# Rounding the inner values of the feed-forward blocks to e5m2 on ScalarE in place of VectorE

## The chip, the cores and the metric

The kernel runs on one core of one Trainium2 chip. The core has five engines that work side by side and wait for each other through semaphores: TensorE (PE in the profile, PEld for its weight loads), VectorE (DVE), ScalarE (ACT), GpSimd (POOL) and SyncE (SP), which issues most DMAs. Each engine takes its instructions in the order in which they were written. The metric is the device time of one execution in microseconds; lower is better.

## The reference, cut to what matters

The model has two layers over 16 images of 48 x 48 pixels and 96 channels (2304 tokens an image). Each layer is a selective scan over the pixels in four directions, followed by a feed-forward block whose operands are rounded to an 8-bit float of 5 exponent and 2 mantissa bits (e5m2):

```python
EXP_MUL, MAN_MUL = (5, 2)
EXP_ACC, MAN_ACC = (5, 10)
q_mul = lambda x: _float_quantize(x, EXP_MUL, MAN_MUL)
q_acc = lambda x: _float_quantize(x, EXP_ACC, MAN_ACC)

def _qlinear(x, W, b):
    y = q_acc(jnp.einsum('bsk,nk->bsn', q_mul(x), q_mul(W)))
    return q_acc(y + q_mul(b))
h = jax.nn.relu(_qlinear(x, W1, b1))
y = _qlinear(h, W2, b2)
```

The inner values `h` have 384 channels a token. They are rounded to 16 bits after the product and after the bias, pass the relu, and are rounded to e5m2 (`q_mul`) as operand of the second product. That last rounding is what the change touches.

## The kernel before

**The scan.** The scans of all images and both layers make one long row of 9216 steps, laid out by `scans`. A step works on a tile of 128 rows by 768 pixels. ScalarE makes the decay `a` by an exp into PSUM (L633, two buffers), GpSimd makes `b` (L639), VectorE runs the scan (L696), the result is multiplied into `hc` (L700), and TensorE folds four `hc` tiles into the output (L663). `hc` has eight buffers. Where the scan's chunk is not the last of its direction, ScalarE copies the last column into `carry` (L706). In the order of the code, step n issues: pieces of other work, scan n (with its product), carry n, exp n+2, GpSimd's `b` of n+3, folds.

**Who multiplies.** The product at L700 goes to VectorE or to GpSimd. A ledger with one account an engine decides, step by step, before anything runs:

```python
here = load["gp"] + 2 * 1.82 > load["ve"] + 1.81 + SPARE
load["gp"] += 1.82 if here else 2 * 1.82
load["ve"] += 2.76 if here else 1.81
```

If `here`, VectorE scans in place and multiplies; otherwise it scans into another tile and GpSimd multiplies. Other work on the two engines enters its cost through `self.ve(us)` and `self.gp(us)`.

**The other work.** Everything besides the scan (norms, convolutions, projections, feed-forward) is written as generators that yield a weight after each piece. A phase is 288 steps; in it the generators of another image advance in proportion to the steps done. In half of the phases the other work is `middle` (the end of layer 0 and the start of layer 1 of an image); in the others it is `final` of one image (the end of layer 1) and `first` of another. After the last scan, the last image's `final` runs alone.

**The feed-forward block.** `feed_forward` (from L970) runs 18 items a block, three for each of six stretches of 384 tokens, as a pipe of three stages: `hidden` (L981, TensorE, into one of two PSUM buffers), `rounded` (L994 copies PSUM to 16 bits, L995 adds the bias and applies the relu in place, both on ScalarE) and `packed`, which after the third item of a stretch rounds the whole 128 x 3 x 384 tile `h1` into `hq` (L1000). `piped` calls the stages of one time in reverse, so that a stretch's `packed` is written ahead of the next stretch's first `rounded`. The second product (L1010) reads `hq`.

Of the kernel before, what the change touches and what calls it, by code (L numbers as in the profile page):

```python
# [16 lines left out]
AF = mybir.ActivationFunctionType  # L17
# [13 lines left out]
SUB = 384  # L31
# [106 lines left out]
class Net:  # L138
# [831 lines left out]
    def feed_forward(self, t, x):  # L970
        nc = self.nc
        w8, b1, b2 = self.ff[t]
        xn = yield from self.norm(x, 1e-5)
        xq = yield from self.channels_first(xn, F8, "xq")
        hq = self.bigt([128, 3, L], "hq", F8)
        h1 = {}

        def hidden(n, _):
            q, m = divmod(n, 3)
            o = self.pst()  # L980
            nc.tensor.matmul(  # L981
                o[:, :SUB],
                lhsT=w8[:DM, m * 128 : (m + 1) * 128],
                rhs=xq[:, q * SUB : (q + 1) * SUB],
                start=True,
                stop=True,
            )
            return o

        def rounded(n, o):  # L990
            q, m = divmod(n, 3)
            if m == 0:
                h1[q] = self.work.tile([128, 3, SUB], F16, name="h1", tag="w3")
            nc.scalar.copy(h1[q][:, m, :], o[:, :SUB])  # L994
            nc.scalar.activation(h1[q][:, m, :], h1[q][:, m, :], AF.Relu, bias=b1[:, m : m + 1])  # L995

        def packed(n, _):
            q, m = divmod(n, 3)
            if m == 2:
                nc.vector.tensor_copy(hq[:, :, q * SUB : (q + 1) * SUB], h1[q], saturate=False)  # L1000
                self.ve(1)

        yield from self.piped(3 * NQ, 0.8, hidden, rounded, packed, by=1)

        def product(q, _):
            o = self.pst()
            for i in range(TQ):
                at = (TQ * q + i) * 128
                for m in range(3):
                    nc.tensor.matmul(  # L1010
                        o[:, i * DM : (i + 1) * DM],
                        lhsT=hq[:, m, at : at + 128],
                        rhs=w8[:, HID + m * DM : HID + (m + 1) * DM],
                        start=(m == 0),
                        stop=(m == 2),
                    )
            return o

        y1 = self.bigt([128, NT, DM], "y1", F16)

        def half(q, o):
            nc.scalar.copy(self.rows(y1, q), o[:, : TQ * DM])

        yield from self.piped(NQ, 1, product, half)

        def biased(q, _):
            o = self.pst()
            nc.tensor.matmul(o[:, : TQ * DM], lhsT=self.ident16, rhs=self.rows(y1, q), start=True, stop=False)
            nc.tensor.matmul(o[:, : TQ * DM], lhsT=self.ones16, rhs=b2, start=False, stop=True)
            return o  # L1030

        yield from self.piped(NQ, 0.9, biased, half)

        def added(q, _):
            o = self.pst()
            nc.tensor.matmul(o[:, : TQ * DM], lhsT=self.ident, rhs=self.rows(x, q), start=True, stop=False)  # L1036
            nc.tensor.matmul(o[:, : TQ * DM], lhsT=self.ident16, rhs=self.rows(y1, q), start=False, stop=True)
            return o

        def put(q, o):  # L1040
            nc.scalar.copy(self.rows(x, q), o[:, : TQ * DM])

        yield from self.piped(NQ, 0.9, added, put)
# [171 lines left out]
```

## Time and profile before

| | |
|---|---|
| time, median of 3 runs | 26079.37 us (26070.98 to 26080.56) |
| the profiled execution's own time | 26086.89 us |
| its span, first to last instruction | 26085.1 us |
| mean granted TensorE clock | 0.754 |
| first scan starts at, last scan starts at | 221.8 us, 25878.7 us |
| L1000 on VectorE | 192 instructions, 259.0 us |
| idle time of VectorE just before L1000 | 138.9 us |
| L994 and L995 on ScalarE | 576 each, 269.8 and 354.0 us |
| ScalarE's table loads, each | 1.283 us |

The page gives the busy time of each engine and its share of the span. Such a share is a mean over stages with different limits. A group of instructions is told by its line, engine, operation and tiles; behind it stand its count, its busy time, the mean of one, and the idle time of the engine just before these instructions with what ended it. A window is a stretch of the span, in us from its start, with the busy time of each engine in it. A timeline lists instructions by their start, with the idle time before each and its releaser in square brackets.

### The profile page before, as it was taken

How to read it: one execution, taken by the hardware profiler on the slowest of the kernel's cores; microseconds unless marked ns; L12 is line 12 of the kernel's file. 1: busy time of each engine (PE TensorE's matmuls, PEld its weight loads, DVE VectorE, ACT ScalarE, POOL GpSimd, SP SyncE). 2: the span in 40 equal slices, each digit the busy share in tenths (PEclk: the TensorE clock that was granted, in tenths of full speed). 3: DMA queues.
4: the chain of work that ended last, by engine and by line, in shares of the span. 5: the costliest groups of instructions: out<-in, count | busy, mean ns of one | idle time of the engine just before them, and what ended most of it. 6: DMA issues, size and time to landing. Idle time of an engine off the chain costs nothing. (4 is left out here: it accounts for less than half of the span.)

```text
span 26085.1 us, 239798 instructions
## 1 busy us (share of the span) xinstructions
PE 18748.3 (72%) x70912; PEld 7359.5 (28%) x70912; DVE 22554.4 (86%) x16250; ACT 15281.8 (59%) x26690; POOL 22797.0 (87%) x13136
## 2 busy tenths in 40 slices
PE   6777667777677766777677866778766777667766
PEld 2223223222222222232222322223222332223222
DVE  6888888888888888888988889888888888988886
ACT  4566555666555565556655566655666555665554
POOL 6888889888888898888998889888899888988886
PEclk7777778777777777787777877778777877778776
DMA  5566566665566565665656656555665555665563
GB/s 194 217 220 224 200 220 227 222 221 209 213 221 222 218 216 209 217 224 219 227 205 218 220 218 231 206 211 219 222 228 216 206 215 221 231 220 204 211 228 140
DMA packets 1297666, 5614.99 MB, mean 215 GB/s; under 512 B 238176, under 2 KB 238176, under 8 KB 1277664
## 3 DMA queue, kind: packets, MB, share of 16 engines
q1 hardware_dynamic: 1219232, 5555.73, 58.4%
q10 hardware_dynamic: 77120, 43.93, 0.6%
q8 instruction: 558, 9.14, 0.1%
q14 instruction: 756, 6.19, 0.1%
HBM read 4707.93 MB, written 891.22 MB: 215 GB/s over the span
## 5 line engine op out<-in xcount | busy, mean ns | idle before, releaser
L639 POOL TENSOR_TENSOR b<-d,bc 128x768 f32<-128x768 f32 x9216 | 16488.9, 1813 | 733.4 <-DVE a L696 699.2
L633 ACT ACTIVATE a<-d,l_a 128x768 f32<-128x768 f32 x9216 | 8317.2, 904 | 3330.9 <-DVE hc L700 2437.2
L696 DVE TENSOR_TENSOR_SCAN a<-a,carry,b 128x768 f32<-128x768 f32 x4374 | 7924.9, 1812 | 887.4 <-ACT a L633 532.2
L663 PE MATMUL py<-hc,fold_sb 128*32 128x384 f32 x36864 | 6237.0, 644 | 2138.1 <-POOL hc L700 1457.3
L700 DVE TENSOR_TENSOR hc<-a,bc 128x768 f32<-128x768 f32 x6408 | 6138.7, 958 | 1254.7 <-PE py L663 637.2
L700 POOL TENSOR_TENSOR hc<-h,bc 128x768 f32<-128x768 f32 x2808 | 5089.8, 1813 | 1713.7 <-DVE h L696 1374.7
L696 DVE TENSOR_TENSOR_SCAN a<-a,b 128x768 f32<-128x768 f32 x2034 | 3557.8, 1749 | 484.6 <-ACT carry L706 244.9
L696 DVE TENSOR_TENSOR_SCAN h<-a,carry,b 128x768 f32<-128x768 f32 x1770 | 3192.2, 1807 | 161.2 <-ACT a L633 89.2
L706 ACT COPY carry<-a 128x1 f32<-128x1 f32 x4119 | 654.6, 159 | 4321.5 <-DVE hc L700 4309.9
L663 PEld LDWEIGHTS py<-hc,fold_sb 128*32 128x32 f32 x36864 | 1200.5, 125 | 6562.0 <-issue 2424.4
L329 PE MATMUL pst<-dts,wpack_sb 24*128 24x384 f32 x2304 | 1446.3, 772 | 1015.5 <-ACT dl L561 985.1
L696 DVE TENSOR_TENSOR_SCAN h<-a,b 128x768 f32<-128x768 f32 x1038 | 1809.6, 1746 | 72.1 <-ACT carry L706 69.8
L437 PE MATMUL pst<-e,dg 128*128 128x384 f32 x5184 | 1802.2, 497 | 0.0
L543 POOL TENSOR_TENSOR du<-dl,u 128x768 f32<-128x768 f32 x576 | 1043.6, 1812 | 598.5 <-DMA dd<-du 283.8
L437 PE MATMUL pst<-wxa,dg 128*128 128x384 f32 x3456 | 1219.2, 502 | 28.6 <-DMA dg<-taps_l1a 22.8
L437 PEld LDWEIGHTS pst<-e,dg 128*128 128x128 f32 x5184 | 952.2, 190 | 862.3 <-issue 267.3
L329 PE MATMUL pst<-xt,wpack_sb 96*128 96x384 f32 (+1 forms) x1536 | 805.7, 661 | 503.2 <-ACT wxb L472 273.2
L329 PEld LDWEIGHTS pst<-dts,wpack_sb 24*128 24x128 f32 x2304 | 587.0, 281 | 1890.2 <-ACT dl L561 1369.3
L651 PE MATMUL py<-first,l_skip 128*128 128x384 f32 x1152 | 689.9, 690 | 537.2 <-ACT yt L676 481.5
L651 PE MATMUL py<-first,ident 128*128 128x384 f32 x1152 | 711.3, 710 | 506.5 <-ACT yt L676 431.7
L329 PE MATMUL pst<-y,centre 128*128 128x384 f32 (+1 forms) x1536 | 853.7, 715 | 272.7 <-ACT y L937 223.8
L329 PE MATMUL pst<-u,wpack_sb 128*128 128x384 f32 (+1 forms) x2304 | 857.1, 518 | 188.7 <-ACT u L508 81.5
(167 smaller groups left out, 17714.6 us busy)
## 6 DMA issues: line engine op xcount, KB each, us to landing
bc<-bc SPq DMA_DIRECT2D x3072, 768.0 KB, 6.7
d<-dd SPq DMA_DIRECT2D x2304, 768.0 KB, 6.1
dd<-dl SPq DMA_DIRECT2D x192, 1152.0 KB, 8.0
dd<-du SPq DMA_DIRECT2D x576, 384.0 KB, 4.4
y<-yt SPq DMA_DIRECT2D x576, 384.0 KB, 2.4
u<-u SPq DMA_DIRECT2D x96, 1152.0 KB, 5.4
first<-u SPq DMA_DIRECT2D x288, 384.0 KB, 3.2
first<-y SPq DMA_DIRECT2D x288, 384.0 KB, 3.2
```

The source lines that it names most:

```text
L329: nc.tensor.matmul(img(o[: w.shape[1], :SUB]), lhsT=w, rhs=y, start=(k == 0), stop=(k == len(terms) - 1))
L437: nc.tensor.matmul(img(o[:, :SUB]), lhsT=dg[:n, k, :], rhs=img(p[:n], PW)[:, PQ * q + i : PQ * q + i + PQ, j : j + HW], start=(k == 0), st ...
L543: nc.gpsimd.tensor_tensor(du, dl[:, cs], u[j][:, cs], ALU.mult)
L633: nc.scalar.activation(a, of(n)[0][:, 0, :], AF.Exp, scale=rates[t][:, pair, j, i, g : g + 1])
L639: nc.gpsimd.tensor_tensor(b, d[:, 1, :], bc[:, 0, :], ALU.mult)
L651: nc.tensor.matmul(py[:, q, :SUB], lhsT=self.skip[t][:, j, :] if pair == 0 else self.ident, rhs=firsts[group][:, q * SUB : (q + 1) * SUB], ...
L663: nc.tensor.matmul(py[32 * k : 32 * k + 32, q, :SUB], lhsT=self.fold, rhs=(hcs[n + k] if q == 0 else hcs.pop(n + k))[:, q * SUB : (q + 1) ...
L696: nc.vector.tensor_tensor_scan(way(h), way(a), way(b), start, ALU.mult, ALU.add)
L700: (nc.vector if here else nc.gpsimd).tensor_tensor(hc, h, cc, ALU.mult)
L706: nc.scalar.copy(kept["carry"][:, at : at + 1], h[:, last : last + 1])
```

## The change

One instruction moves from VectorE to ScalarE. ScalarE's `activation` with `Identity` copies its input and rounds it to the type of the output, e5m2; it stands where VectorE's cast stood, and on ScalarE that is behind the relu that it reads and ahead of the next item's L994. The entry of 1 us in VectorE's account goes too, so that the ledger decides some later products otherwise.

```diff
         def packed(n, _):
             q, m = divmod(n, 3)
             if m == 2:
-                nc.vector.tensor_copy(hq[:, :, q * SUB : (q + 1) * SUB], h1[q], saturate=False)
-                self.ve(1)
+                nc.scalar.activation(hq[:, :, q * SUB : (q + 1) * SUB], h1[q], AF.Identity, saturate=False)
 
         yield from self.piped(3 * NQ, 0.8, hidden, rounded, packed, by=1)
```

## The prediction

> **What bounds the kernel now.** I read the page's busy shares first, then the groups by line and shape, then the windows of the stage that the diff touches, then the timeline inside one window. The chain of waits is not used: it accounts for 0% of the span on every engine.
>
> ```profile
> PE 18748.3 (72%) x70912; PEld 7359.5 (28%) x70912; DVE 22554.4 (86%) x16250; ACT 15281.8 (59%) x26690; POOL 22797.0 (87%) x13136
> ```
>
> VectorE (DVE) and GpSimd (POOL) share the load at 86% and 87%; ScalarE (ACT) looks free at 59%. But the change lives only where a feed-forward block makes its inner values, and there the shares differ. For each window below I took the stretch from an image's first L981 matmul to its last L995 relu: two from the first layer (the scan's middle phases), two from the second layer (with the next image's first part), then the two last images. Columns: length, then busy us (x instructions) of PE, PEld, DVE, ACT, POOL, clock, DMA share, GB/s.
>
> ```profile
> 7801.30:7845.60 44.30, 20.53 (x100) 5.08 (x97) 35.39 (x27) 32.62 (x64) 36.69 (x22) 0.62 0.37 135
> 8634.10:8676.00 41.90, 18.89 (x100) 4.97 (x96) 35.26 (x27) 32.85 (x64) 37.31 (x22) 0.62 0.43 155
> 9347.70:9393.40 45.70, 22.36 (x111) 5.40 (x110) 43.88 (x32) 33.88 (x54) 42.90 (x26) 0.63 0.63 234
> 10143.20:10192.90 49.70, 26.09 (x110) 6.15 (x111) 47.73 (x35) 35.20 (x56) 46.80 (x27) 0.57 0.58 208
> 25683.50:25775.90 92.40, 50.25 (x180) 10.55 (x182) 90.20 (x65) 56.87 (x107) 90.38 (x52) 0.63 0.52 195
> 26050.10:26085.10 35.00, 18.94 (x103) 9.34 (x101) 8.12 (x6) 25.14 (x55) 0.00 (x0) 0.70 0.10 26
> ```
>
> The second layer's windows are held by VectorE, 96% busy (43.88 of 45.70, 47.73 of 49.70). In the first layer's windows nobody is full: VectorE 80 to 84%, GpSimd 83 to 89%, ScalarE 74 to 78%. The timeline shows why:
>
> ```profile
> 15097.29 0.19 ACT L706 COPY carry<-h 128x1 f32<-128x1 f32 x1 [1.04 <-DVE h L696]
> ...
> 15100.19 0.90 ACT L633 ACTIVATE a<-d,l_a 128x768 f32<-128x768 f32 x1
> 15101.03 0.47 ACT L994 CAST h<-pst 128x384 f16<-128x384 f32 x1
> ...
> 15102.18 1.35 DVE L1000 CAST hq<-h 128x1152 fp8e5<-128x1152 f16 x1 [2.22 <-ACT h L995]
> 15102.54 0.61 ACT L995 ACTIVATE h<-h,l_b 128x384 f16<-128x384 f16 x1
> ...
> 15103.45 1.75 DVE L696 TENSOR_TENSOR_SCAN h<-a,b 128x768 f32<-128x768 f32 x1
> 15105.11 1.74 DVE L696 TENSOR_TENSOR_SCAN a<-a,b 128x768 f32<-128x768 f32 x1
> 15105.23 0.19 ACT L706 COPY carry<-h 128x1 f32<-128x1 f32 x1 [2.07 <-DVE h L696]
> ```
>
> VectorE's pack stands ahead of the next scan and waits 2.22 us for ScalarE's relu; ScalarE's carry copy then waits 2.07 us for that scan. Two steps take 15105.23 - 15097.29 = 7.94 us, a closed loop over both engines.
>
> **Price of the pack on each engine.** Groups by shape (count | busy, mean ns | idle before, releaser):
>
> ```profile
> L571 ACT ACTIVATE dl<-dl 128x2304 f32<-128x2304 f32 x192 | 407.7, 2123 | 2.2
> ...
> L995 ACT ACTIVATE h<-h,l_b 128x384 f16<-128x384 f16 x576 | 354.0, 615 | 18.7
> ...
> L1000 DVE CAST hq<-h 128x1152 fp8e5<-128x1152 f16 x192 | 259.0, 1349 | 138.9 <-ACT h L995 135.4 <-ACT carry L706 3.5
> ...
> L364 ACT ACTIVATE sq<-xm 128x864 f32<-128x864 f32 x128 | 114.5, 908 | 19.7 <-DVE xm L356 19.7
> ```
>
> VectorE loses 192 casts of 1.35 us, 259 us busy; on a full VectorE each takes 1.27 us (15102.18 to 15103.45). No ScalarE row has 1152 elements. L364 and L571 give (2123 - 908)/1440 = 0.844 ns an element, so 908 + 288 x 0.844 = 1151 ns; L995, which has a bias vector, gives 615 + 768 x 0.844 = 1263 ns as the upper end. The added instruction has no bias vector like L364, so I take 1.15 us: 192 x 1.15 = 221 us busy. Neighbours on ScalarE overlap by some 0.06 us (exp 0.90 at 15100.19, next at 15101.03), so 1.09 us each when it is full: 6.5 us a window of six packs.
>
> **What else moves.** The deleted ledger entry of 1 us lets VectorE take more hc products: an added one costs 2.76 - 1.81 = 0.95 there and saves 1.82 on GpSimd, so 192/(0.95 + 1.82) = 69; the changed program's order of instructions has 66 (6474 against 6408 at L700 on VectorE). That is 2.06 a window: VectorE +1.8 us (some 0.88 each, from hc to next scan), GpSimd -3.7 us. No DMA is added or moved past. The pack waits only for ScalarE's own relu. Queued behind it are the next L994 (which frees the PSUM buffer that L981 waits for), the carry copy and the exp of two steps on, which the scan after next waits for. So an exp may come 1.09 us late; cover is the exp's lead. In a step of 2.72 us (scan and hc) ScalarE has exp 0.84 and one item of 1.02 = 1.86, with a pack 2.95: 0.2 over in one step of three, and a whole step of lead to absorb it. PE's folds of hc stand behind L981 on its queue; a fold of four hc that comes 1.09 us later is covered by the other four of hc's eight buffers, four steps of 2.7 us. Without the exp's lead each pack would show as 1.09 us on VectorE (the slower rival).
>
> **The sum, by window.** Sixteen images pass two blocks each, 32 windows: 16 of the first layer, 14 of the second beside a next image's first part, image 14's, and image 15's after the last scan.
> - First layer, 16 windows, mean 43.1 us. ScalarE becomes fullest: 32.7 + 6.5 = 39.2 us; VectorE falls to 35.3 - 7.6 + 1.8 = 29.5, GpSimd to 33.3. With the pack off VectorE the 7.94 us loop is gone: the scan follows hc at once and carry is ready when ScalarE comes. An engine that bounds today reaches 96%, so 39.2/0.96 = 40.8: -2.3 each, -37. Ends: 0 and the bare 39.2 (-3.9).
> - Second layer, 14 windows, mean 47.7. New loads: VectorE 38.1 and 41.9, ScalarE 40.4 and 41.7, GpSimd 39.2 and 43.1; the largest, 40.4 and 43.1, is 5.3 and 6.6 below today. Three engines within 6% of each other behind short buffers will not reach 96%; I take half, -3.0 each, -42. Ends: 0 and -5.9.
> - Image 14's window (92.4 us, GpSimd 98%): GpSimd's -3.7.
> - Image 15's window runs alone, with ScalarE back to back: +6.5, nothing hides it.
>
> Sum: -37 - 42 - 4 + 6.5 = -76. The profiled execution took 26086.9 (span 26085.1, 1.8 around it), so 26011; the median of the runs shown is 7.5 lower: **26003 us**. About 180 us of VectorE's 259 thus buy nothing, since ScalarE or GpSimd is next.
>
> **Rivals.**
> - *Nothing left over ScalarE (floors).* All windows reach the fullest engine's load: -62 - 83 - 4 + 6.5 = -142, 25937. For it: ScalarE's waits today are for VectorE, which gets lighter. Against: no window is above 96%.
> - *ScalarE merely takes over the bound.* First layer 0, second -1: -14 - 4 + 6.5 = -11, 26068. For it: after the change ScalarE's 39.2 is already within 4 us of 43.1, and the same stage differs by 2.4 us (44.3 against 41.9) with the scan pattern alone. Against: the broken loop.
> - *Slower: the pack delays every exp.* In the second layer ScalarE's idle 11.8 to 14.5 us a window is waiting for hc, which frees its PSUM buffer, so it may not be fillable; then each pack adds its 1.09 to the scans there: 14 x 6.5 + 6.5 = +98, 26177. It decides where two short steps (scan without hc, 1.72 us) follow a pack. For it: VectorE's largest wait of all is for the exp (738 us in 427 waits). Against: the lead worked out above. The Trainium skill, page "ScalarE: Activation LUTs", section "Rules for kernel authors", speaks for this side: elementwise work belongs on VectorE, up to three times faster there. The row disagrees for this cast: 1.35 us on VectorE against 1.15 estimated on ScalarE. By the page's factor the removed cast would have cost VectorE only some 0.4 us, and the sum would go to this rival.
> - *Table loads.* If Identity needed a table of its own, two loads of 1.283 us a pack, up to 493 us: 26500. Against: the Identity rows L358 and L378 (1116 each) have no load beside them.
>
> **How the numbers follow.** Chances: forecast 0.50, floors 0.12, takeover 0.21, slower 0.15, table loads 0.02. The forecast's own range is 25965 to 26045; 0.08 of it lies within 0.2% of before (52 us, about what a measurement of this kernel tells from no change). Faster 0.42 + 0.12 = 0.54; within 0.08 + 0.20 = 0.28; slower 0.17 + 0.01 = 0.18. Range 25930 to 26100: floors and takeover inside, the slower cases left out.
>
> **What would show it.** Right: L1000 at 1.15 us x192 on ScalarE; first-layer windows near 41 us with ScalarE over 93% and its wait for scan and hc almost gone; second-layer windows near 44.5; 66 hc moved; the last window 6.5 longer. Wrong: ScalarE still idle over 15% in the windows while VectorE waits for exp (L633), or a window length unchanged.

## The result

The changed kernel takes 25954.85 us (median of 4 runs, 25942.37 to 25960.17), the kernel before 26075.17 us over its runs: ratio 0.9955, 95% interval 0.9938 to 0.9973, 120 us faster. The forecast was 26003 us, faster by 76. The profiled execution has a span of 25940.4 us, 144.7 under that of before. The page's busy shares hardly move:

```profile
PE 18725.5 (72%) x70912; PEld 7347.3 (28%) x70912; DVE 22388.9 (86%) x16124; ACT 15456.2 (60%) x26882; POOL 22687.6 (87%) x13070
```

The windows say more. These are of the changed kernel, cut as before (an image's first L981 matmul to its last L995 relu), three of the first layer, two of the second, and image 14's. Columns: length, then busy us (x instructions) of PE, PEld, DVE, ACT, POOL, clock, DMA share, GB/s.

```profile
7800.10:7838.40 38.30, 16.22 (x91) 5.09 (x88) 31.48 (x24) 36.12 (x67) 35.15 (x21) 0.72 0.38 137
8611.50:8652.30 40.80, 19.26 (x91) 5.19 (x88) 33.88 (x26) 37.49 (x69) 36.13 (x21) 0.65 0.42 158
15000.60:15041.20 40.60, 18.52 (x91) 5.08 (x88) 33.44 (x25) 37.09 (x68) 35.62 (x21) 0.61 0.42 155
10109.90:10154.60 44.70, 23.80 (x118) 5.52 (x115) 43.10 (x32) 39.49 (x62) 43.83 (x26) 0.66 0.65 231
9320.40:9365.60 45.20, 25.43 (x124) 6.26 (x124) 43.24 (x32) 39.64 (x62) 44.04 (x26) 0.63 0.61 221
25528.60:25622.10 93.50, 42.78 (x163) 8.77 (x162) 86.57 (x62) 60.72 (x113) 87.23 (x50) 0.67 0.52 194
```

In the first layer ScalarE (ACT) went from 74 to 78% of the window to 91 to 94%, and the mean window of the 16 from 43.0 to 40.8 us, with 37.2 us of ScalarE's work in it; in the second VectorE (DVE) is still 96% busy, but GpSimd (POOL) is at 97 to 98%; the mean of the 14 windows went from 47.4 to 43.5 us. The timeline shows the place where the closed loop was, one stretch of tokens in a first-layer window, with ScalarE's and VectorE's lines alone:

```profile
15015.11 0.14 ACT L706 COPY carry<-a 128x1 f32<-128x1 f32 x1
15015.28 0.91 ACT L633 ACTIVATE a<-d,l_a 128x768 f32<-128x768 f32 x1
...
15016.10 0.96 DVE L700 TENSOR_TENSOR hc<-a,bc 128x768 f32<-128x768 f32 x1
15016.12 1.15 ACT L1000 ACTIVATE hq<-h 128x1152 fp8e5<-128x1152 f16 x1
15016.98 1.75 DVE L696 TENSOR_TENSOR_SCAN h<-a,b 128x768 f32<-128x768 f32 x1
15017.18 0.46 ACT L994 CAST h<-pst 128x384 f16<-128x384 f32 x1
...
15018.68 0.61 ACT L995 ACTIVATE h<-h,l_b 128x384 f16<-128x384 f16 x1
...
15019.93 0.92 ACT L633 ACTIVATE a<-d,l_a 128x768 f32<-128x768 f32 x1
...
15020.95 1.77 DVE L696 TENSOR_TENSOR_SCAN a<-a,b 128x768 f32<-128x768 f32 x1 [2.22 <-ACT a L633]
```

VectorE's scan at 15016.98 follows its product at once; the rounding runs beside it. ScalarE shows no idle time in brackets. Now it is VectorE that waits, 2.22 us for an exp that stands behind a rounding, two items and a copy of `yt`: ScalarE has become the bound. VectorE's waits in the whole window (waiter, releaser, us in total, times, longest):

```profile
DVE a L696 <- ACT a L633: 5.9, 5, 2.2
DVE hc L700 <- PE pst L981: 0.5, 1, 0.5
```

Windows cut by time have a flaw that matters below: when ScalarE falls behind, VectorE gets through more steps in the same window (in the first layer 14.8 on average where it was 13). So I also measured by steps, from the traces: the time from the start of scan 140 to that of scan 160 of a phase in the first layer (mean of 16 phases) and from scan 100 to scan 122 in the second (mean of 14), and the durations of the instructions that stand between the same steps in each engine's order, added up.

| us | first layer: time | VectorE | ScalarE | GpSimd | second layer: time | VectorE | ScalarE | GpSimd |
|---|---|---|---|---|---|---|---|---|
| before | 60.3 | 53.9 | 45.4 | 52.4 | 59.6 | 59.8 | 41.9 | 57.0 |
| the change | 55.2 | 48.1 | 52.1 | 48.3 | 54.2 | 53.8 | 48.5 | 53.3 |
| move, entry kept | 55.4 | 45.9 | 52.2 | 52.5 | 52.8 | 51.8 | 48.5 | 57.3 |
| entry dropped alone | 62.6 | 56.1 | 45.4 | 48.2 | 61.8 | 61.8 | 41.8 | 53.3 |
| one item later on VectorE | 56.3 | 53.9 | 45.4 | 52.4 | 58.8 | 59.8 | 41.9 | 57.0 |
| late stage on VectorE | 54.3 | 53.9 | 44.6 | 52.4 | 58.7 | 59.6 | 41.1 | 57.3 |
| empty piece alone | 59.6 | 53.9 | 44.7 | 52.3 | 59.4 | 59.7 | 41.1 | 57.3 |
| relu writes e5m2, pieces moved | 52.1 | 47.9 | 45.3 | 48.6 | 53.2 | 53.7 | 42.6 | 53.5 |
| relu writes e5m2, pieces kept | 50.8 | 45.9 | 45.4 | 52.5 | 52.4 | 51.7 | 41.8 | 57.1 |
| rounding twice on ScalarE | 61.6 | 48.1 | 59.1 | 48.2 | 58.7 | 53.8 | 55.5 | 53.4 |

The sums are good for comparing rows, but they are not shares of the time: neighbours on an engine overlap a little, and a sum counts that twice. Counted once, the second layer's VectorE is 57.7 us before and 52.1 in the change, and the first layer's ScalarE in the change 47.9 in place of 52.1. A sum can also exceed the time because an engine does part of the work of these steps before or after them, out of buffers: GpSimd's 57.3 in 52.8 is 55.9 counted once. The change's account: 16 x (55.2 - 60.3) = -82, 14 x (54.2 - 59.6) = -76, the end of the program behind the last scan +9.5 (206.4 to 215.9 us); together -148 of the measured -144.7. The rest of the program gives back 4 net, in pieces of both signs.

The ledger does more than its count tells: the net is 66 products, but by the traces 3268 of the 9216 steps have their product on the other engine than before. The run with the entry dropped alone and the one with two roundings have the same assignment as the change; the move with the entry kept has that of the kernel before.

### The profile page after: what moved, and what is told of

Read it like the earlier page. It is cut to its first block, busy times and chain, and to the rows that moved or that the text cites. A ratio compares the mean times of both kernels' runs of the same rounds, so it can differ in the third digit from the quotient of the medians.

```text
span 25940.4 us, 239820 instructions
## 1 busy us (share of the span) xinstructions
PE 18725.5 (72%) x70912; PEld 7347.3 (28%) x70912; DVE 22388.9 (86%) x16124; ACT 15456.2 (60%) x26882; POOL 22687.6 (87%) x13070
## 3 DMA queue, kind: packets, MB, share of 16 engines
q1 hardware_dynamic: 1219232, 5555.73, 58.7%
## 5 line engine op out<-in xcount | busy, mean ns | idle before, releaser
L633 ACT ACTIVATE a<-d,l_a 128x768 f32<-128x768 f32 x9216 | 8316.5, 904 | 3192.7 <-DVE hc L700 2357.8
L700 DVE TENSOR_TENSOR hc<-a,bc 128x768 f32<-128x768 f32 x6474 | 6201.8, 958 | 1303.2 <-PE py L663 673.9
L700 POOL TENSOR_TENSOR hc<-h,bc 128x768 f32<-128x768 f32 x2742 | 4969.6, 1812 | 1601.2 <-DVE h L696 1284.4
L696 DVE TENSOR_TENSOR_SCAN a<-a,b 128x768 f32<-128x768 f32 x2069 | 3621.2, 1750 | 582.5 <-ACT carry L706 309.0
L696 DVE TENSOR_TENSOR_SCAN h<-a,carry,b 128x768 f32<-128x768 f32 x1739 | 3137.8, 1807 | 139.9 <-ACT carry L706 74.4
L696 DVE TENSOR_TENSOR_SCAN h<-a,b 128x768 f32<-128x768 f32 x1003 | 1750.3, 1747 | 76.3 <-ACT carry L706 65.0
```

What stands on the lines that cost most here:

```text
L633: nc.scalar.activation(a, of(n)[0][:, 0, :], AF.Exp, scale=rates[t][:, pair, j, i, g : g + 1])
L696: nc.vector.tensor_tensor_scan(way(h), way(a), way(b), start, ALU.mult, ALU.add)
L700: (nc.vector if here else nc.gpsimd).tensor_tensor(hc, h, cc, ALU.mult)
```

## The experiments

All ratios are against the kernel before, run on the same chip at the same time, with their 95% intervals.

**The ledger entry alone** (the rounding stays on VectorE):

```diff
                 nc.vector.tensor_copy(hq[:, :, q * SUB : (q + 1) * SUB], h1[q], saturate=False)
-                self.ve(1)
```

> The rounding stays on VectorE, only the ledger entry of 1 us is dropped. Theory A: VectorE gets 1.8 us more in each window of the second layer, where it is the bound, and the loop with ScalarE stays in the first layer's: 26075 plus about 25, 26100. Rival B: most of the gain without the move, about 25980.

26175.51 us, ratio 1.0036 (1.0024 to 1.0049): slower by 101 us. In the table VectorE gets 2.2 and 2.0 us more in the two layers' stretches, and these get 2.3 and 2.2 longer, 37 + 31 of the 89 us by which the profiled execution is longer; some 20 more are elsewhere. Theory A had put the loss at 25 us, all of it in the second layer. Dropping the entry is a loss, and rival B falls: the gain of the change is not the ledger's.

**The move with the entry kept:**

```diff
-                nc.vector.tensor_copy(hq[:, :, q * SUB : (q + 1) * SUB], h1[q], saturate=False)
+                nc.scalar.activation(hq[:, :, q * SUB : (q + 1) * SUB], h1[q], AF.Identity, saturate=False)
                 self.ve(1)
```

> The rounding on ScalarE, but VectorE's ledger entry of 1 us kept, so that the 66 products stay on GpSimd. Theory A (occupancy and loop: the cast leaves VectorE, the closed loop with ScalarE's relu is gone, the ledger only shares out what is won): the first layer's windows gain as in the change, about 5 us each, since ScalarE bounds them at 37 us and GpSimd has only 37; the second layer's windows stay under GpSimd's old load (42.9 and 46.8 us) and gain 2 to 3 us in place of 6; time about 25990. Rival B (the gain is the ledger's: a better share and another scan pattern): close to the kernel before, 26060 or more.

25904.59 us, ratio 0.9932 (0.992 to 0.9945). The first layer is as in the change (55.4), as theory A said. But the second layer gains more than in the change, 52.8 against 54.2, where 2 to 3 us in place of 6 were expected. Two first-layer windows and one of the second:

```profile
14125.90:14167.10 41.20, 21.43 (x100) 5.49 (x97) 31.77 (x23) 37.13 (x69) 38.59 (x23) 0.54 0.41 146
14946.50:14988.40 41.90, 20.52 (x100) 5.45 (x96) 32.13 (x23) 37.24 (x69) 39.64 (x24) 0.58 0.44 157
15656.50:15696.80 40.30, 20.97 (x110) 4.86 (x108) 38.07 (x26) 37.99 (x59) 40.14 (x23) 0.66 0.65 240
```

GpSimd is full (40.14 of 40.30) and VectorE is at 94% (38.07), and yet the stretch is shorter than where VectorE has the 66 products: part of GpSimd's work for these steps is done outside the stretch. Because the interval overlaps with that of the change, both were run once more on one chip:

> The changed kernel once more, beside the next one on the same chip, to measure what the dropped ledger entry is worth. Theory A (VectorE, full in the second layer's windows, is better off with the entry, since the 66 products stay on GpSimd, whose backlog is absorbed outside the windows): the change is 30 to 50 us slower than the move with the entry kept; rival (the first difference was chance): within 15.

> The move with the ledger entry kept once more, beside the changed kernel on the same chip. Theory A: 25905, 30 to 50 us under the change. Rival: within 15 us of it.

The change 25942.99 us (25926.51 to 25954.24, ratio 0.995, 0.9936 to 0.9964), the entry kept 25883.95 (25872.1 to 25932.92, ratio 0.9931, 0.9918 to 0.9943): 59 us between the medians, 50 the first time, on different chips then. The intervals still touch, and the two profiled executions of the second pair are only 3 us apart (that of the entry kept is the slowest of its five). But both pairs of medians, the table (52.8 against 54.2, both times) and the run with the entry dropped alone point the same way. Of the difference 16 us are in the two stretches; where the rest lies is not shown.

**The wait without the move.** The rounding stays on VectorE, but is issued one item later, when its relu has long ended; the last of a block is not delayed, and no piece of other work is added (the later ledger entry moves 86 of the 9216 products):

```diff
             q, m = divmod(n, 3)
-            if m == 2:
-                nc.vector.tensor_copy(hq[:, :, q * SUB : (q + 1) * SUB], h1[q], saturate=False)
+            for p in ([q - 1] if m == 0 and q else []) + ([q] if n == 3 * NQ - 1 else []):
+                nc.vector.tensor_copy(hq[:, :, p * SUB : (p + 1) * SUB], h1[p], saturate=False)
                 self.ve(1)
```

> The rounding stays on VectorE with its ledger entry; each stretch's rounding is issued one item later, the last one not, and no piece of the other work is added or moved. Theory A (in the first layer the closed loop with the relu is what costs): steps 140 to 160 of the first layer's phases fall by about 5 us each as in the run with the late stage, the second layer's by 0 to 1, nothing else moves: about 25990. If the late stage won by its added piece alone (theory E): 26075.

25982.84 us, ratio 0.9966 (0.9954 to 0.9978). Its timeline in a first-layer window, with ScalarE's and VectorE's lines alone:

```profile
15010.29 0.61 ACT L995 ACTIVATE h<-h,l_b 128x384 f16<-128x384 f16 x1
15010.50 0.96 DVE L700 TENSOR_TENSOR hc<-a,bc 128x768 f32<-128x768 f32 x1
...
15011.37 1.34 DVE L1000 CAST hq<-h 128x1152 fp8e5<-128x1152 f16 x1
15011.49 0.16 ACT L706 COPY carry<-a 128x1 f32<-128x1 f32 x1 [0.58 <-DVE hc L700]
15011.68 0.91 ACT L633 ACTIVATE a<-d,l_a 128x768 f32<-128x768 f32 x1
15012.52 0.47 ACT L994 CAST h<-pst 128x384 f16<-128x384 f32 x1
15012.63 1.75 DVE L696 TENSOR_TENSOR_SCAN h<-a,b 128x768 f32<-128x768 f32 x1
```

The cast starts at once behind the product, and the copy of the carry waits 0.58 us where one waited 2.07 in the kernel before. Over the whole execution VectorE's wait for the relu falls from 135.4 us to half:

```profile
L1000 DVE CAST hq<-h x192: 1325/1343/1355, 1393.7 to 25942.6; 128x1152 fp8e5<-128x1152 f16 x192
...
its engine sat idle before it (us, times) until:
  ACT h L995: 69.1, 58
```

In a first-layer block the idle time of VectorE before its six casts falls from 7.0 to 3.2 us, of which 2.1 stand before the last cast, which is not delayed. The first layer's stretch falls by 4.0 us with VectorE's load unchanged, where the move with the entry kept wins 4.9; the second layer's by 0.8. So in the first layer the wait is most of what the move wins; in the second, where VectorE is full, taking the cast away is what helps. Of this run's gain 64 + 11 us are in the two stretches; a further 51 of the profiled execution's 126 are elsewhere and not explained (the profiled execution is also the fastest of six, 22 us under their median).

**The same with a further stage**, which came first and proved impure:

```diff
-        yield from self.piped(3 * NQ, 0.8, hidden, rounded, packed, by=1)
+        yield from self.piped(3 * NQ, 0.8, hidden, rounded, lambda n, v: v, packed, by=1)
```

> The rounding stays on VectorE with its ledger entry, but is issued one item later, so that the relu that it reads is long done: the wait goes and the occupancy stays. Theory A says that in the first layer's windows the loop is what costs: VectorE's 5 to 8 us of waits for the relu a window go, the windows end near GpSimd's and VectorE's 36 to 37 us, 3 to 5 us less each; the second layer's windows, where VectorE is full, do not change: about 26010. If occupancy alone counts (theory C), nothing changes: 26075.

25902.13 us, ratio 0.9933 (0.9921 to 0.9946), some 100 us more gain than theory A gave. The first layer's 54.3 fits it. But the traces show 109 us of gain in steps 240 to 264 of the phases, where no rounding is: the added stage puts one more piece into the generator and shifts all pieces behind it. That alone was tried next:

```diff
-        yield from self.piped(3 * NQ, 0.8, hidden, rounded, packed, by=1)
+        yield from self.piped(3 * NQ, 0.8, hidden, rounded, packed, lambda n, v: v, by=1)
```

> The kernel before with one empty piece behind the rounding in each block: the loop stays, the later pieces of other work are shifted by one. The run with the late stage gained 108 us in steps 240 to 264 of its phases, where no rounding is. If that is the shift: the same gain there alone and the first layer's windows as before, about 25975. If that stretch gained from the loop (theory A alone): 26075.

26012.01 us, ratio 0.9974 (0.9963 to 0.9985). The rounding's stretches stay (59.6 and 59.4), and steps 240 to 264 gain 106 us; the other steps gain and lose, and cancel but for 10. An empty piece is worth more than half of the change (68 us against 120). It has no instruction of its own, but by the trace it moves 2571 of the 9216 products to the other engine, besides the pieces behind it. Which of the two that stretch gains from was not tried, so the cause stays open.

**ScalarE's load doubled**, by the same rounding done twice in the changed kernel:

```diff
                 nc.scalar.activation(hq[:, :, q * SUB : (q + 1) * SUB], h1[q], AF.Identity, saturate=False)
+                nc.scalar.activation(hq[:, :, q * SUB : (q + 1) * SUB], h1[q], AF.Identity, saturate=False)
```

> The changed kernel with ScalarE's rounding done twice: 192 x 1.15 us more on ScalarE. Theory A (ScalarE is full in the first layer's windows, 37 of 40.6 us, and close to it in the second's): the first layer's grow by 6.5 us each, 104, the second layer's by about 2, 28, the last image by 7: about 26095. If ScalarE's load is hidden: only the last image's 7, 25962.

26123.67 us, ratio 1.0017 (1.0008 to 1.0025). Against the change, whose schedule it shares, the stretches grow by 6.4 us in the first layer and 4.5 in the second. 16 x 6.4 + 14 x 4.5 + 4.2 behind the last scan = 169.6, the difference of the spans being 26110.2 - 25940.4 = 169.8. That it comes out so closely is chance: other steps of the first layer's phases lose 21 us more, and other steps of the second's gain 20. A window of either layer:

```profile
15097.50:15143.80 46.30, 19.75 (x91) 5.22 (x88) 33.57 (x25) 42.86 (x73) 35.86 (x21) 0.60 0.36 135
15810.10:15859.80 49.70, 25.84 (x124) 6.39 (x124) 44.26 (x32) 45.27 (x67) 44.89 (x26) 0.62 0.58 214
```

ScalarE's added 7.0 us (59.1 against 52.1) appear almost whole in the first layer, 6.4: it was full there after the change. In the second it had about 2 us to spare, and theory A's 2 us a stretch was too little.

**No rounding of its own.** The relu writes e5m2; the 16-bit rounding between the bias and e5m2 is left out. First with the stage and the ledger entry gone:

```diff
-            nc.scalar.activation(h1[q][:, m, :], h1[q][:, m, :], AF.Relu, bias=b1[:, m : m + 1])
+            nc.scalar.activation(
+                hq[:, m, q * SUB : (q + 1) * SUB], h1[q][:, m, :], AF.Relu, bias=b1[:, m : m + 1], saturate=False
+            )
...
-        yield from self.piped(3 * NQ, 0.8, hidden, rounded, packed, by=1)
+        yield from self.piped(3 * NQ, 0.8, hidden, rounded, by=1)
```

> The relu writes e5m2 directly, no separate rounding instruction is left on any engine (the 16-bit rounding between bias and e5m2 is left out). Theory A, in which ScalarE now bounds the first layer's windows (37 of 40.6 us): they fall by another 4 us each to GpSimd's 36, the second layer's by up to 1, the last image by 7: about 25870. If ScalarE's added load is hidden (theory D: the windows are held by waits, not by ScalarE's load): only the last image's 7, about 25945.

25951.13 us, ratio 0.9954 (0.994 to 0.9968): no faster than the change, which looks like theory D. The table contradicts: the stretches gained another 3.1 and 1.0 us, and the last image its 9.6. So some 72 us were lost elsewhere. There is one piece less in each block, and 584 products are on the other engine than in the change; no run separates the two. With the third stage kept, empty but for the ledger entry, all products are as in the kernel before:

```diff
         def packed(n, _):
-            q, m = divmod(n, 3)
-            if m == 2:
-                nc.vector.tensor_copy(hq[:, :, q * SUB : (q + 1) * SUB], h1[q], saturate=False)
+            if n % 3 == 2:
                 self.ve(1)
```

> The relu writes e5m2 directly (the 16-bit rounding between bias and e5m2 is left out), with the ledger entry and the third stage kept, so that no piece and no product moves against the kernel before. Theory A: against the move with the entry kept, the first layer's windows lose ScalarE's 6.5 us and fall 2 to 4 us each, the second layer's stay, VectorE being full there, and the last image loses its 7 to 9: about 25850. If ScalarE's load is hidden everywhere: 25897.

25823.08 us, ratio 0.9904 (0.989 to 0.9918). The first layer's stretch is 50.8, 4.6 under the move with the entry kept, the second's 0.4: as theory A said, ScalarE's time counts in the first layer and hardly in the second. Against the run with the cast one item later, with the same load of ScalarE and the cast gone from VectorE, the first layer gains 5.5 us more (56.3 to 50.8), of which up to 2.1 are the wait that was left there. So VectorE's time counts in the first layer too, once the wait is gone; the move cannot win it, since ScalarE is full by then.

```profile
14905.40:14943.00 37.60, 18.79 (x100) 4.95 (x96) 31.73 (x23) 32.17 (x66) 37.60 (x22) 0.64 0.47 172
15612.20:15650.30 38.10, 21.45 (x110) 5.22 (x108) 37.24 (x27) 33.32 (x54) 37.94 (x22) 0.69 0.68 250
```

GpSimd is now full in both (37.60 of 37.60, 37.94 of 38.10). Last, this one with the empty piece:

> The relu writes e5m2 directly (the 16-bit rounding between bias and e5m2 is left out), ledger entry kept, and one empty piece more in each block. If the gain of the empty piece (68 us on the kernel before, in stretches without any rounding) has nothing to do with the rounding, it adds up: about 25755. If it came from the same waits: 25823.

25781.04 us, ratio 0.9887 (0.9874 to 0.9901), 1.1% under the kernel before and the fastest of all. That is 42 us under the run without the empty piece, with which it did not share a chip, where 68 were expected: the two gains add up for the most part. The profiles agree: steps 240 to 264 take 95 us less than in the run without the empty piece.

## Why the prediction came out as it did

The direction and the first layer's mechanism held. The time lay in the range of 25930 to 26100, but 10 us below the forecast's own range (25965 to 26045) and closer to the rival of the floors (25937): the gain was 120 us where 76 were forecast. By the profiles the terms came out as -82 and -76 for the layers (-37 and -42 forecast), +1 for image 14 (-4), +9.5 for image 15 (+6.5), and 3 given back in the rest.

- *Price of the rounding: right.* The rows of the changed kernel:

```profile
L995 ACT ACTIVATE h<-h,l_b 128x384 f16<-128x384 f16 x576 | 354.1, 615 | 18.7
...
L1000 ACT ACTIVATE hq<-h 128x1152 fp8e5<-128x1152 f16 x192 | 220.8, 1150 | 1.2
```

  1150 ns against 1151 worked out. The Trainium skill, page "ScalarE: Activation LUTs", section "What ACT_TABLE_LOAD costs", gives 186 ns and 0.833 ns an element for an activation with immediate scale and bias, an estimate of 1146; the trace agrees, with a median of 1147. No table load was added (376 at L633 and 190 at L571, as before), so that rival is out.
- *First layer: right in mechanism, half in size.* The step that failed is "First layer, 16 windows, mean 43.1 us", forecast at -2.3 and measured at -5.1. It took the change of a window's length for the time that is gained, but the window opens and closes with the block's own work. Before, part of the waiting for relus fell behind the window's end, where the last cast stood (2.4 of 7.0 us a block); and after, VectorE does 15 steps inside a window that held 13. The window itself came out at 40.8 us, as forecast, and that was partly luck: ScalarE's load in it is 37.2 us, not 39.2 (of the six roundings one stands behind its end), and ScalarE is busy for 91% of it, not 96%. The two misses cancel.
- *Second layer: the step that failed is "I take half, -3.0 each", with its reason that three engines so close to each other "will not reach 96%".* Measured -5.4 by steps (-3.9 by windows), nearly the whole of VectorE's loss of 6.0 us. The three engines hardly get in each other's way: with overlaps counted once, VectorE is busy for 52.1 of 54.2 us, 96%, where it was 97% before the change, GpSimd for 52.3, and ScalarE still had 2 us to spare.
- *The ledger: counted right (66 products), judged wrong.* I booked GpSimd's 3.7 us as relief and VectorE's 1.8 as part of the floor. The runs with and without the entry show that in the second layer's stretches VectorE's time is the scarce one and part of GpSimd's work is done outside: by the medians the dropped entry costs 50 to 59 us of what the move wins.
- *Image 14's window: forecast -3.7, measured +1.1* (93.50 against 92.40; by steps 212 to 250 of that phase +0.6). With the entry kept, where GpSimd is not relieved, these steps take 4.6 us less than before. So GpSimd's relief is not what counts there; what does was not tried.
- *The last image: forecast +6.5, measured +9.5, and +7.0 in the repeat of the change.* ScalarE alone, behind the last scan:

```profile
25921.51 0.61 ACT L995 ACTIVATE h<-h,l_b 128x384 f16<-128x384 f16 x1
25922.16 1.16 ACT L1000 ACTIVATE hq<-h 128x1152 fp8e5<-128x1152 f16 x1
25923.23 0.68 ACT L1021 CAST y<-pst 128x288 f16<-128x288 f32 x2
```

  The rounding reads what the relu has just written and starts 0.65 us after it, where another instruction followed after 0.52; with its own 1.07 it takes a slot of 1.20 us in place of 1.09, so 7.2 for six. The prediction left out that VectorE's last cast, 1.35 us behind the last relu, goes: from the first L981 to the end of the last rounding the block grows by 5.8 us (20.6 to 26.4), in the repeat too. Behind it the closing part takes 17.1 us against 14.8, at a granted clock of 0.80 against 0.85 over that part; since the run without a rounding of its own has 16.7 us there (0.81), ScalarE's rounding is not needed for it, and its cause stays open. What is left of the 9.5, 1.3 us, lies ahead of the block and is -0.9 in the repeat.
- *The slower rival is out.* Exps do come late: 5.9 us of VectorE's waits in the first-layer window shown. But there VectorE has the time (33.4 us of work in 40.6); in the second-layer window from 10109.9 it waits 0.4 us for exps in all.

## What to carry to other kernels

Where two in-order engines hand work back and forth, look for an instruction that stands in one queue and waits for the other's newest result; issuing it one item later won 4.0 of the move's 4.9 us in the first layer, without moving any work to another engine, and is a smaller edit than a move. Count an engine's load by a fixed piece of work (steps), not by a window in time that the work itself opens and closes. In a schedule that is laid out by hand weights, a change of one piece or one ledger entry moved thousands of products here and 20 to 106 us in stretches that were not meant, so hold the layout fixed when a move is measured, and tune it afterwards on its own.

## What the runs showed that was not expected

An empty piece of work, with no instruction in it, made the kernel before 0.26% faster (ratio 0.9974, 0.9963 to 0.9985), as much as all of it in a stretch where no rounding is (106 us in steps 240 to 264). And GpSimd can have 55.9 us of work in a stretch of 52.8 us: it takes 56.2 us for its instructions of these steps, almost without a gap, and so falls 3.4 us behind the scans, which the buffers between the engines allow.
